# Adjacency tiles kept only in the passes that read them, three more page buffers and a fourth round of first pages in a two-layer graph and expert kernel

## The chip, the cores and the metric

The kernel runs on one core of a Trainium2 chip, in one launch. The metric is the device time of that launch in microseconds (us), taken as the median of a few runs. Times inside the kernel are from one profiled execution, counted from the start of its span. The engines are named as in the profile: PE is the tensor engine (PEld its weight loads), DVE the vector engine, ACT the scalar engine, POOL GpSimd, SP the sync engine, which issues most of the DMA transfers.

## What is computed

The input is 128 graphs of 64 nodes with 256 features, so 8192 rows (`tokens`), and a dense 64x64 adjacency for each graph. Two layers follow each other. Cut to what matters here:

```python
# layer 0
n = layernorm(x);  agg = eps * n + adj @ n
x = x + silu(rmsnorm(agg @ W1 + b1)) @ W2 + b2          # 256 -> 1024 -> 256
n = layernorm(x);  top6 of 64 experts by n @ gate_w.T   # softmax over the six scores
x = x + LN(n + (sum_k score_k * n @ lattice[expert_k]) @ out_w.T + out_b)
# layer 1
n = layernorm(x);  h = LN(n)
x = x + n + relu((adj @ h) @ W_rel + b_rel + h @ W_root)
n = layernorm(x);  top2 of 8 experts
x = x + sum_k p_k * (relu(n @ W1[e_k] + b1[e_k]) @ W2[e_k] + b2[e_k])
```

All of it is in float32. The adjacency is used twice, once in each layer, and the expert sums are sparse: each row goes to six of 64 matrices of 256x256 in layer 0, and to two of eight two-step networks in layer 1.

## The kernel before

The rows are worked on in 32 blocks of 256 (`NB`, two tiles of 128 rows, four graphs). There are four passes, each a `staggered` loop that writes out the order of PE, DVE and ACT by hand (`manual_schedule`); the order of SP's transfers is the scheduler's.

**Layer 0, dense and routing.** For each block `load0` (L787) brings the rows and `load_adjacency` (L745) the four transposed adjacency matrices, as two 64x64 corners of a 128x128 tile for each of the two tiles. `aggregate`, `hidden`, `scale` and `project` make the dense part. Then `choose`, `count` and `slots` give every row its six experts and a place in each expert's list, and GpSimd scatters copies of the row to the table `r0x` in memory (`Router.send`, L419, six copies of two tiles for each block). The last sends end at 614.87 us.

**Layer 0's pages.** An expert's list is read in pages of 128 rows. `page_table` (L443) makes the order of pages on the device: first up to `R` full pages of every expert in turn, then the other full pages, then what is left over, with small rests as half pages. `R` is 3 (the argument of the router before the tuple of likely counts, L977). Twelve pages (`EARLY`) go ahead in buffers of their own (`early0` to `early5`, L1079). Then `run` (L1200) works through 188 pairs of pages and 7 pairs of half-page groups: `fetch` (L1138) loads a pair into a `px` buffer, of which there are 22 (L1140), up to twelve pairs ahead of its use in program order; `flip` transposes it on PE; `apply` (L1173) multiplies by the expert's matrix and DVE scales the result back into the same `px` buffer (L1192); `Router.reply` (L426) lets GpSimd scatter each page's results to the rows of the answer table `r0y`. A `px` buffer is free again when both replies of its pair have landed. For the first 64 pairs ACT also writes a filler page for an expert (`fill_end`). Behind the usual pages stand two branches with spare pages, entered only if the routing needs them.

**Layer 1, dense and routing.** `load_y` (L1340) loads a block's six answers for each row from `r0y`, 1.57 MB a block, in three `y` buffers, four blocks ahead. `mixture` (L1360) sums and transposes them on PE; `fold` (L1381) lets DVE add two of the six first, for blocks after the seventh. A load of `y` must not overtake the replies that it reads. For the blocks below `READY` (6) the loads are declared independent of the replies of pages from `R` x 64 on (the group `r0last`, L431 and L1346): rows of these first blocks lie at the head of each expert's list, so they are in the first `R` rounds. To make sure, `look_back` (L205) notes after `READY` blocks how many rows each expert has, and `page_table` asks for the spare pages, which end in a wait, if some expert has more than the first rounds hold. Loads for later blocks wait for all replies. `load3` (L1354) brings `x1` and the adjacency again; `convolve_b` (L1474) uses it. Rows go to the experts' table `r1x` by GpSimd (`send1`).

**Layer 1's pages** are the last pass; GpSimd adds their results to the output.

The adjacency tiles: four tiles `at0` to `at3` of 1024 bytes a partition are made once, at L740 to L743, in the pool `const`, which lives for the whole kernel. They are cleared once by GpSimd, since loads write only their diagonal corners, and a block `b` uses tile `b % 4` in both layers. Since the tiles are the same, the loads of layer 1's first four blocks stand, in the program that is built, at the end of layer 0's dense pass in SP's queue.

Of the kernel before, what the change touches and what calls it, by code (L numbers as in the profile page):

```python
# [9 lines left out]
F32 = mybir.dt.float32  # L10
# [9 lines left out]
P = 128  # L20
# [71 lines left out]
def chain(blocks, make, key=None):  # L92

    key = key or make.__name__

    def advance(b, n=1):
        B = blocks[b]
        if key not in B:
            B[key] = make(b)
        for _ in range(n):  # L100
            if next(B[key], B) is B:
                break

    return advance
# [562 lines left out]
def two_layer_gnn_moe_kernel(ctx: ExitStack, tc: tile.TileContext, a: dict, out: bass.AP):  # L667
    nc = tc.nc
    x_in, adjT = a["x"], a["adjT"]
    N, D = x_in.shape  # L670
# [4 lines left out]
    T = 2  # L675
    C = T * P
    NB = N // C
    E0 = a["L0_ffn_lattice_weights"].shape[0]
    H0 = a["L0_gnn_W1"].shape[1]
    KH = H0 // P  # L680
    K0 = 6
    E1, F1, _ = a["L1_ffn_W2"].shape
    EARLY = 12
    READY = 6
    FIRST = 4
    FOLD = 2
    LOOK = 20
# [3 lines left out]
    const = ctx.enter_context(tc.tile_pool(name="const", bufs=1))  # L691
    small = ctx.enter_context(tc.tile_pool(name="small", bufs=3))
    counts = ctx.enter_context(tc.tile_pool(name="counts", bufs=3))
    dram = ctx.enter_context(tc.tile_pool(name="dram", bufs=1, space=bass.MemoryType.DRAM))
# [21 lines left out]
    def load_matrix(pool, name, engine=nc.scalar):  # L716

        t = pool.tile([P, a[name].shape[0] // P, a[name].shape[1]], F32, name="m_" + name)
        engine.dma_start(out=t, in_=a[name].rearrange("(k p) f -> p k f", p=P))
        return t  # L720
# [16 lines left out]


    adjacency = []
    for i in range(4):  # L740
        at = const.tile([P, T, P], F32, name=f"at{i}")
        nc.gpsimd.memset(at, 0.0)
        adjacency.append(at)  # L743

    def load_adjacency(b):  # L745
        at = adjacency[b % 4]
        for g in range(2):
            nc.sync.dma_start(out=at[g * G:(g + 1) * G, :, g * G:(g + 1) * G],
                              in_=adjT[2 * b * T + g:2 * (b + 1) * T:2].rearrange("t m n -> m t n"))
        return at  # L750
# [3 lines left out]
    W = D + 2  # L754
# [20 lines left out]
    with tc.tile_pool(name="c0", bufs=1) as c0, \  # L775
            tc.tile_pool(name="work0", bufs=2) as work, \
            tc.tile_pool(name="ph0", bufs=4, space=PSUM) as ph_pool, \
            tc.tile_pool(name="ps0", bufs=2, space=PSUM) as psum, \
            tc.tile_pool(name="pm0", bufs=1, space=PSUM) as pmix:
        mean = c0.tile([P, P], F32, name="mean")  # L780
        nc.gpsimd.memset(mean, 1.0 / H0)
        route = pmix.tile([P, 2, T, E0], F32, name="route")
# [4 lines left out]
        def load0(b):  # L787
            B = blocks[b]
            B["x"] = x = x_view[:, b % 4 * T:(b % 4 + 1) * T, :]
            nc.sync.dma_start(out=x, in_=by_tile(x_in[ts(b, C), :]))  # L790
            B["at"] = load_adjacency(b)
# [156 lines left out]
        def place(b):  # L948
            send(b, 0)
            if b == READY - 1:  # L950
                r0.look_back()
# [3 lines left out]
        def send(b, k):  # L955

            B = blocks[b]
            r0.release(k, *B["w"], B["xs"])
            r0.send(B["row"], B["xs"], b > LOOK, (k,))
# [14 lines left out]
        aggregate(0)  # L974
        rest = lambda f: lambda b: f(b) if b else None

        r0 = Router(tc, const, small, dram, N, D, E0, K0, T, P, 14 * P, 4, "r0", 3, ((K0 * N // P - EARLY) // 4 * 4 + 4, E0 // 2 - 4), True)  # L977
        r1 = Router(tc, const, small, dram, N, D, E1, 2, T, 2 * P, N, 4, "r1", 1,
                    (N // P // 2 - E1 // 2, E1 // 4, E1 - 1), True, total=out, like=r0)
        assert W == r0.W  # L980
# [1 line left out]
        H, R, Q, V, S, Y = (chain(blocks, f) for f in (choose, residual_a, square_sum, normalize, slots, scale))  # L982
# [133 lines left out]
    with tc.tile_pool(name="wx0", bufs=3, reuse_waits="tile") as wx, \  # L1116
# [20 lines left out]

        def fetch(j):  # L1138
            Q = pairs[j]
            Q["px"] = px = wx.tile([P, 2, W], F32, name="px", bufs=22)  # L1140
            if j >= npair:
                regs["row"] = r0.load(2, 4 * (j - npair), ENG.SP)
                for i in range(4):
                    q, h = i // 2, i % 2 * P // 2
                    r0.fetch_rows(regs["row"][i], px[h:h + P // 2, q:q + 1, :], P // 2)
                return
            for q in range(Q["n"]):
                i = 2 * j + q
                if i % 4 == 0:
                    regs["row"] = r0.load(0, i, ENG.SP)  # L1150
                r0.fetch(i, regs["row"][i % 4], px[:, q:q + 1, :])
# [21 lines left out]
        def apply(j):  # L1173
# [17 lines left out]
            for q in range(n):  # L1191
                nc.vector.tensor_scalar(px[:, q, :D], py[:, q, :], px[:, q, D + 1:D + 2], None, op0=ALU.mult)  # L1192
                r0.reply(2 * j + q, px[:, q, :], px[:, q, :D])


        stages = ((-12, fetch), (0, apply),
                  (-2, lambda j: flip(j) if j < 4 or j >= npair else None),
                  (-3, lambda j: flip(j) if 4 <= j < npair else None))
# [23 lines left out]
    wx = ctx.enter_context(tc.tile_pool(name="wx1", bufs=2, side="right", reuse_waits="tile"))  # L1222
# [102 lines left out]
    with tc.tile_pool(name="c3", bufs=1, reuse_waits="tile") as c3, \  # L1325
# [5 lines left out]
        ln_g, ln_b, gamma, beta, bg = (over[x] for x in ("ln_g", "ln_b", "gamma", "beta", "bg"))  # L1331
        w_rel, w_root = (c3.tile([P, KD, D], F32, name="m_" + x) for x in ("rel", "root"))
        wg = load_matrix(c3, "L1_ffn_Wg")
        one = c3.tile([P, P], F32, name="one")
        nc.vector.memset(one, 1.0)
        blocks = [dict() for _ in range(NB)]
# [3 lines left out]
        def load_y(b):  # L1340
            B = blocks[b]
            B["y"] = y = work.tile([P, T, K0, D], F32, name="y", bufs=3)
            for t in range(T):
                d = nc.sync.dma_start(out=y[:, t],
                                      in_=r0.answer[ts(b * T + t, P * K0), :].rearrange("(p k) d -> p k d", k=K0))
                if b < READY:  # L1346
                    tc.declare_no_dep(d.ins, group="r0last", reason="in the first pages, or waited for above")
# [6 lines left out]
        def load3(b):  # L1354
            B = blocks[b]
            B["x1"] = x1 = work.tile([P, T, D], F32, name="x1", bufs=3)
            nc.sync.dma_start(out=x1, in_=by_tile(x1_dram[b]))
            B["at"] = load_adjacency(b)
# [22 lines left out]
        def fold(b):  # L1381

            B = blocks[b]
            B["n"] = K0
            if b > READY + 1:
                B["n"] = n = K0 - FOLD
                y = B["y"]
                nc.vector.tensor_add(y[:, :, :FOLD], y[:, :, :FOLD], y[:, :, n:])
# [177 lines left out]
        for i in (-4, -3, -2):  # L1566
# [50 lines left out]
            (3, count1),  # L1617
            (4, ahead((-3, lambda: down(-4, 0, (0,))), (-2, lambda: up(-3)))),
            (-3, fold),
            (0, A),  # L1620
            (3, S),
# [27 lines left out]
    with tc.tile_pool(name="pt4", bufs=2, space=PSUM, reuse_waits="tile") as pt_pool, \  # L1649
# [26 lines left out]
        def run(order):  # L1676
            order = tuple(order)
            staggered(len(order), [(lag, lambda n, f=f: f(order[n]))
                                   for lag, f in ((-2, fetch), (0, then(flip1)), (1, finish), (0, then(up)))])
# [44 lines left out]
```

## Time and profile before

| what | value |
|---|---|
| median of three runs | 1968.87 us (1968.59 to 1971.76) |
| the profiled execution, its own time | 1970.99 us |
| its span | 1969.2 us |
| granted clock of PE, mean | 0.973 |
| busy in the span | PE 1852.8, PEld 1613.4, DVE 1146.4, ACT 1002.0, POOL 1134.5 us |
| layer 0, dense and routing: PE until | 583 us |
| layer 0's pages: PE's last product ends | 1097.28 us |
| layer 0's pages: GpSimd's last reply ends | 1131.87 us |
| layer 1, dense and routing: PE until | 1477 us |
| layer 1's pages: last add starts | 1956.42 us |

The page of the profile gives busy time by engine, the same in 40 slices of 49.2 us, and groups of like instructions. A group line names the line of code, the engine, what is written and read, the count, the busy time and the mean of one in ns, then the idle time of the engine just before them and what ended most of it. Windows give the busy time of each engine in a stretch, with the number of instructions in brackets. A wait line reads: who waited, for whom, us in total, how many times, the longest. A timeline line reads: start, duration, engine, line, operation, output and input, how many in a row, and in square brackets the idle time before it and what ended it.

### The profile page before, as it was taken

Reading aid. Unit: us, or ns where it says so; the run is one execution under the profiler, and the core shown is the slowest. Engines: PE = TensorE matmul, PEld = TensorE weight load, DVE = VectorE, ACT = ScalarE, POOL = GpSimd, SP = SyncE. Lnnn points to the kernel's source line nnn. Section 1 sums busy time; section 2 is a strip of 40 time slices with the busy share of each in tenths; the row PEclk is TensorE's granted clock in tenths of the full one; section 3 lists DMA queues with packets and bytes.
Section 4 is the critical chain, followed back from the end, with each engine's and each line's share of the span. In section 5 each row is a group of like instructions: output and inputs, shape, how many; then the busy total and the mean of one; then the engine's idle time right before and its main releaser. Section 6 shows DMA issues by size and latency. Waiting matters only on the chain. (4 is left out here: it accounts for less than half of the span.)

```text
span 1969.2 us, 35306 instructions
## 1 busy us (share of the span) xinstructions
PE 1852.8 (94%) x9906; PEld 1613.4 (82%) x9906; DVE 1146.4 (58%) x4256; ACT 1002.0 (51%) x2047; POOL 1134.5 (58%) x1114
## 2 busy tenths in 40 slices
PE   7999999999966899999999899999987999999996
PEld 6888888888845777888877788888876888888885
DVE  5899999999975333344433379999962222222221
ACT  5888888988841222222222266666642333333332
POOL 1377777777677677777777724444443444434443
PEclk9999999999967999999999899999988999999998
DMA  5134555553376988766666799778425666666653
GB/s 139 63 131 143 164 162 163 159 165 131 118 258 216 301 257 264 213 213 206 207 208 191 295 307 337 272 258 281 155 88 129 161 133 130 131 134 130 129 108 48
DMA packets 253085, 359.49 MB, mean 183 GB/s; under 512 B 53176, under 2 KB 210504, under 8 KB 252880
## 3 DMA queue, kind: packets, MB, share of 16 engines
q1 hardware_dynamic: 175904, 210.74, 36.0%
q0 software_dynamic: 62736, 135.21, 23.2%
q10 hardware_dynamic: 14240, 11.12, 1.8%
q8 instruction: 90, 1.47, 0.3%
q14 instruction: 115, 0.94, 0.2%
HBM read 193.27 MB, written 166.03 MB: 182 GB/s over the span
## 5 line engine op out<-in xcount | busy, mean ns | idle before, releaser
L419 POOL DMA_INDIRECT r0x<-xs,r0row x384 | 388.0, 1010 | 216.2 <-ACT lat L883 113.6
L426 POOL DMA_INDIRECT r0y<-px x390 | 378.7, 971 | 122.9 <-DMA r0y<-px 52.2
L1188 PE MATMUL py<-lat,pxT 128*128 x1616 | 385.6, 383 | 21.0 <-ACT pxT L1162 17.7
L436 POOL DMA_INDIRECT out_x<-py_s,px x131 | 202.8, 1548 | 282.5 <-DVE py_s L1322 179.3
L1192 DVE TENSOR_SCALAR px<-py,px 128x256 f32<-128x256 f32 x390 | 171.0, 480 | 306.9 <-PE py L1188 300.7
L1188 PEld LDWEIGHTS py<-lat,pxT 128*128 128x128 f32 x1616 | 293.1, 191 | 60.3 <-ACT pxT L1162 22.2
L1162 ACT COPY pxT<-pt 128x512 f32<-128x512 f32 x188 | 109.7, 586 | 345.3 <-PE pt L1159 241.0
L1292 ACT ACTIVATE phid<-ph,pw 128x256 f32<-128x256 f32 (+1 forms) x264 | 122.0, 462 | 293.0 <-PE ph L1289 180.4
L419 POOL DMA_INDIRECT r1x<-xs,r1row x128 | 134.9, 1054 | 184.1 <-ACT hn L1432 53.9
L894 PE MATMUL ps<-lat 128*128 128x256 f32 x1024 | 240.0, 383 | 0.0
L858 PE MATMUL ph<-lat 128*128 128x256 f32 x1024 | 233.3, 387 | 2.7 <-DVE lat L881 2.0
L1303 PE MATMUL py<-fw,phid 128*128 (+1 forms) x1016 | 232.7, 382 | 0.0
L1289 PE MATMUL ph<-pxT,pw 128*128 128x256 f32 (+1 forms) x1056 | 227.0, 368 | 0.0
L858 PEld LDWEIGHTS ph<-lat 128*128 128x128 f32 x1024 | 195.9, 194 | 29.8 <-issue 2.4
L894 PEld LDWEIGHTS ps<-lat 128*128 128x128 f32 x1024 | 194.3, 192 | 28.3
L1289 PEld LDWEIGHTS ph<-pxT,pw 128*128 128x128 f32 x1056 | 193.0, 190 | 24.7
L1303 PEld LDWEIGHTS py<-fw,phid 128*128 128x128 f32 x1016 | 189.6, 192 | 23.5
L1314 DVE TENSOR_SCALAR p<-p 128x2 f32<-128x2 f32 (+1 forms) x69 | 12.2, 177 | 218.5 <-ACT p L1313 218.5
L1159 PE MATMUL pt<-ident,px 128*128 128x128 f32 x780 | 120.7, 276 | 11.6 <-DMA px<-r0x 11.6
L1320 DVE TENSOR_TENSOR py_s<-py,pb 128x512 f32<-128x512 f32 (+1 forms) x67 | 44.5, 664 | 143.7 <-PE py L1303 141.4
L1159 PEld LDWEIGHTS pt<-ident,px 128*128 128x128 f32 x780 | 97.3, 142 | 36.1 <-issue 10.9
L881 DVE SCALAR_TENSOR_TENSOR lat<-ph,c_L_gnn_b,rms 128x256 f32<-128x256 f32 x256 | 111.9, 476 | 23.0 <-ACT rms L72 22.9
(337 smaller groups left out, 2966.9 us busy)
## 6 DMA issues: line engine op xcount, KB each, us to landing
y<-r0y SPq DMA_DIRECT2D x64, 768.0 KB
px<-r0x SPq DMA_DIRECT2D x376, 129.0 KB
pw<-in_L_ffn_W1b SPq DMA_DIRECT2D x41, 514.0 KB
x<-x SPq DMA_DIRECT2D x64, 256.0 KB
px<-r1x SPq DMA_DIRECT2D x28, 516.0 KB
r0x<-r0filler ACTq DMA_DIRECT2D x64, 129.0 KB
lat<-in_x SPq DMA_DIRECT2D x32, 256.0 KB
lat<-in_L_ffn_lattice_weights SPq DMA_DIRECT2D x8, 1024.0 KB
```

The source lines that it names most:

```text
L419: i = self.nc.gpsimd.indirect_dma_start(out=self.table[:, :], out_offset=bass.IndirectOffsetOnAxis(ap=row[:, t, k:k + 1], axis=0), in_=xs[ ...
L426: d = self.nc.gpsimd.indirect_dma_start(out=self.answer[:, :], out_offset=bass.IndirectOffsetOnAxis(ap=x[:, self.D:self.D + 1].bitcast(I32 ...
L436: i, d = f"{self.name}add{i}", self.nc.gpsimd.indirect_dma_start(out=self.total[:, :], out_offset=bass.IndirectOffsetOnAxis(ap=x[:, self.D ...
L858: nc.tensor.matmul(ph[:, c, :], lhsT=w1[:, k, ts(2 * j + c, P)], rhs=B["aggT"][:, k, :], start=(k == 0), stop=(k == KD - 1))
L881: nc.vector.scalar_tensor_tensor(hT[:, c, :], B["ph", c // 2][:, c % 2, :], b1[:, c:c + 1], B["rms"], op0=ALU.add, op1=ALU.mult)
L894: nc.tensor.matmul(B["po"][:, t, :], lhsT=B["hT"][:, c, ts(t, P)], rhs=w2[:, c, :], start=False, stop=(t == T - 1 and c == KH - 1))
L1159: nc.tensor.transpose(pt[:, k, ts(q, P)], Q["px"][:, q, ts(k, P)], ident)
L1188: nc.tensor.matmul(py[:, q, :], lhsT=xT[q][:, k, ts(h, P)] if parts == 2 else xT[:, k, ts(q, P)], rhs=lat[:, ds(e, 1), k, :].rearrange("p ...
L1192: nc.vector.tensor_scalar(px[:, q, :D], py[:, q, :], px[:, q, D + 1:D + 2], None, op0=ALU.mult)
L1289: nc.tensor.matmul(ph[c - c0][:, :m], lhsT=w[:, k * F1 + c * P:k * F1 + (c + 1) * P], rhs=Q["xT"][:, k, :m], start=(k == 0), stop=(k == KD ...
L1292: nc.scalar.activation(hid[:, c, :m], ph[c - c0][:, :m], AF.Relu, bias=w[:, KD * F1 + c:KD * F1 + c + 1], scale=1.0)
L1303: nc.tensor.matmul(py[:, t, :], lhsT=Q["hid"][:, c, ts(t, P)], rhs=fw2[:, ds(e, 1), c, :].rearrange("p o d -> p (o d)"), start=(c == 0), s ...
```

## The change

The adjacency tiles become tiles of the pools of the two passes that use them, `c0` in layer 0 and `c3` in layer 1. In layer 1 they are new tiles and are cleared again, by DVE. The pool of page buffers has 25 pairs in place of 22, which takes 3 x 2064 bytes a partition; the tiles took 4 x 1024. `R` of layer 0's router is 4 in place of 3 and `READY` 8 in place of 6; the condition of `fold` is written anew and holds for the same blocks as before.

```diff
-    READY = 6
+    READY = 8
...
     adjacency = []
-    for i in range(4):
-        at = const.tile([P, T, P], F32, name=f"at{i}")
-        nc.gpsimd.memset(at, 0.0)
-        adjacency.append(at)
+
+    def clear_adjacency(pool, engine):
+        for i in range(4):
+            at = pool.tile([P, T, P], F32, name=f"at{i}")
+            engine.memset(at, 0.0)
+            adjacency.append(at)

     def load_adjacency(b):
-        at = adjacency[b % 4]
+        at = adjacency[b % 4 - 4]
...
+        clear_adjacency(c0, nc.gpsimd)
         mean = c0.tile([P, P], F32, name="mean")
...
-        r0 = Router(tc, const, small, dram, N, D, E0, K0, T, P, 14 * P, 4, "r0", 3, ((K0 * N // P - EARLY) // 4 * 4 + 4, E0 // 2 - 4), True)
+        r0 = Router(tc, const, small, dram, N, D, E0, K0, T, P, 14 * P, 4, "r0", 4, ((K0 * N // P - EARLY) // 4 * 4 + 4, E0 // 2 - 4), True)
...
-            Q["px"] = px = wx.tile([P, 2, W], F32, name="px", bufs=22)
+            Q["px"] = px = wx.tile([P, 2, W], F32, name="px", bufs=25)
...
         wg = load_matrix(c3, "L1_ffn_Wg")
+        clear_adjacency(c3, nc.vector)
         one = c3.tile([P, P], F32, name="one")
...
-            if b > READY + 1:
+            if b >= READY:
                 B["n"] = n = K0 - FOLD
```

In the program that is built, PE, ACT and POOL have the same instructions in the same order. DVE has four memsets more at the start of layer 1 and notes `r0seen` two blocks later. On SP the eight adjacency loads of layer 1's first four blocks leave the end of layer 0's dense pass and stand one pair after each `x1` load of blocks 0 to 3; from block 4 on some neighbours change places.

## The prediction

> **What bounds the kernel now.** I read the page's slices first. From slice 11 to 22 GpSimd (POOL) stands at 7 in every slice while TensorE (PE) is not always full; after that PE is full and POOL low.
>
> ```profile
> PE   7999999999966899999999899999987999999996
> ...
> POOL 1377777777677677777777724444443444434443
> ...
> L426 POOL DMA_INDIRECT r0y<-px x390 | 378.7, 971 | 122.9 <-DMA r0y<-px 52.2
> ```
>
> The third line is the page's group of replies: GpSimd scatters each finished page of layer 0 to its tokens' rows, 390 times. Busy 971 ns each; the timeline shows one starting every 1.275 us (1128.35, 1129.62, 1130.90), with 0.30 us between them that never shrinks. So a 7 in the slices is a full GpSimd. Next, the stage in windows (columns: window, PE, PE weight load, VectorE, ScalarE, POOL, PE clock, DMA share, GB/s):
>
> ```profile
> 700.00:750.00 50.00, 45.52 (x244) 38.81 (x243) 17.54 (x40) 11.70 (x20) 38.11 (x40) 1.00 0.87 262
> ...
> 850.00:900.00 50.00, 50.00 (x279) 44.10 (x278) 20.34 (x47) 13.65 (x24) 38.10 (x40) 1.00 0.66 206
> ...
> 1000.00:1050.00 50.00, 45.40 (x241) 38.09 (x240) 17.53 (x40) 11.71 (x20) 38.05 (x40) 1.00 0.69 210
> ```
>
> POOL makes 40 replies in each 50 us. A page costs PE six records (two transposes, four products), so PE makes 279/6 = 46.5 pages where it is free, and 40 where it isn't. PE thus gains on POOL from 800 to 970 us and is then held to POOL's pace. What holds it is in the waits of SP's queue between 680 and 1060 us, which fetches the pages:
>
> ```profile
> SPq L652 <- DMA r0y<-px: 168.6, 126, 4.0
> ```
>
> The fetch of pair j waits for the replies of pair j-22, because the `px` buffer is read by them. Counting fetches and replies in the timeline up to one moment, fetches are 39 to 42 pages ahead of replies at every tenth microsecond from 680 to 1060 (22 pairs are 44 pages), and finished pages are ahead of replies by 6 at 800, 19 at 890, 30 at 970, then 30 to 32 until 1080: a full window. The end of the stage, from the timelines of PE, SP and POOL:
>
> ```profile
> 1090.21 7.07 PE L1188 MATMUL py<-lat,pxT 128*128 x32
> ...
> 1097.65 0.83 SPq L1344 DMA_DIRECT2D y<-r0y  x2
> ...
> 1102.53 2.79 PE L1367 MATMUL ps<-ident,y 128*128 128x128 f32 x12 [5.24 <-DMA y<-r0y]
> ...
> 1125.20 1.53 PE L1367 MATMUL ps<-ident,y 128*128 128x128 f32 x12 [0.87 <-DMA y<-r0y]
> ...
> 1130.90 0.97 POOL L426 DMA_INDIRECT r0y<-px  x1 [0.30 <-issue]
> ...
> 1137.49 0.80 SPq L1344 DMA_DIRECT2D y<-r0y  x2
> ```
>
> PE ends its pages at 1097.28, layer 1 starts at once (first `y` load 0.37 us later), and POOL replies on to 1131.87, under layer 1. So the path that sets the time runs: POOL's replies, one buffer window, PE's last page, layer 1. POOL's own end is not on it, except through the `y` load at 1137.49, which waits for the last reply to land (POOL's next instruction waits for the same until 1137.54). From 1125.2 to 1400 PE is full but for 0.14 us.
>
> **What the Trainium skill says.** "Perfetto Trace Analysis", Optimization Strategy: the same gap repeated over a stretch can mean too few buffers for the next tile. The trace agrees: the 126 waits above. "DMA: Bandwidth & Descriptors", Issuing engines are not separate DMA queues: transfers of SP, ScalarE and GpSimd share the same 16 DMA engines. Agrees: with `y` loads and replies together the DMA share is 1.00 to 1.05 in each 5 us window from 1100 to 1130. "TensorE: Matmul & The Clock Gate", What's actually happening: an idle PE falls to half clock. Agrees: granted clock 0.53, 0.50, 0.61 in the three windows from 1100 to 1115, after the 5.24 us gap; the change keeps that gap, so it moves along.
>
> **The change, part by part.**
>
> *Three more `px` pairs (22 to 25).* The window grows by 6 pages. Where it was full, each fetch can go 6 replies earlier: 6 x 1.275 = 7.65 us. PE needs 6 pages more lead to use it; at its gain of (31-6) pages in 170 us that takes 41 us, so even without a better start it has it by about 1011, before the last paced pages near 1063. From there PE works without a wait to 1097.28 (half pages), so its end moves to 1089.6. POOL's end stays near 1132: it never starves but for 1.06 + 2.21 us at 675 to 680, when the 22 pairs had only just filled (fetches 41 ahead at 680); more buffers hardly act there. I take 0; the ends are -3.3 (gap gone) and +3 (gap doubled). **-7.65.**
>
> *Four rounds of pages first, `READY` 8.* The order of pages changes (up to four of an expert before the rest), their number does not. Counted from the reference's inputs: 373 pages and 27 halves under either setting, within the 376 and 28 of the usual pass. The guard that would run the spare passes compares rows of the first `READY` blocks with the first rounds: after 8 blocks the fullest expert has 407 rows, under 4 x 128. So no spare pass. `y` of blocks 0 to 7 now waits for the first 256 pages, whose replies were issued by 960. Block 8 is the first to wait for the last reply; its load went at 1147.19 and would go at 1139.5, still after 1137.5. In the kernel before, block 6's late load cost PE nothing (landed 1144, used 1155), so the gain is 0; left at 6, it would be wanted 7.65 us sooner and still be hidden by the three `y` buffers. **0.** The fold keeps its blocks (`b > 7` and `b >= 8` are the same).
>
> *Adjacency tiles, last part of layer 0.* Eight loads (four blocks, two each) leave SP's queue there. POOL's sends run without a break to 614.87 and set that stage's end. **0.** The four tiles now lie at the head of `c0`, so the six early page pairs lie 4096 bytes lower against the old buffers; the wait for a block's sends goes from the fifth early pair to the sixth. PE stood 9.72 us at that wait, but the early replies could not start before 615 (POOL), nor VectorE evict before its page table was done near 611. **0**; if uncovered, at most those 10 us either way, which POOL takes up.
>
> *Adjacency tiles, layer 1.* Four memsets of 128x256 on VectorE, 272 ns each (row L1168; "VectorE: DVE Perf Modes", Zero memsets can be issued as uint32, gives one cycle per element, 267 ns at its 0.96 GHz): 1.09 us, in 17.95 us of VectorE idleness (1099.3 to 1117.2) and ahead of the first adjacency load. **0**, 1.1 if that cover went. The eight loads now stand in SP's queue between the `y` loads: one pair after each of blocks 0 to 3's `x1`, 0.60 us an issue, 4.8 us in all. Worse, transfers of SP and ScalarE take eight completion semaphores in turn and each waits until the transfer eight before has landed. By the new order `y` of block 2 waits for the end of block 0's second half, block 3's for block 1's, and so on. With the landings of before I get issues at 1107.4, 1114.2, 1119.5 and 1125.8 for blocks 2 to 5, instead of 1103.43, 1109.46, 1115.28 and 1121.70. But the DMA engines take `y` first in, first out, back to back: in the trace's packets the first of those blocks start at 1112.27, 1117.00, 1122.50 and 1127.65. With 1 us from issue to first packet (1097.65 to 1098.64) slack remains: 3.9, 1.8, 2.0 and 0.9 us. So the engines don't run dry; behind SP wait only further loads. What stays is the data: 256 packets of 256 bytes a block at 17 to 18 ns over 16 engines, 0.28 us, three blocks of it ahead of block 3's second half, PE's last wait (1125.20). **+0.9**; ends 0 and, with all four slacks missed by 2 us, +8.
>
> *Carrying on.* From 1150 to 1400 PE is full and POOL at 20 to 25 of 50; waits further on (10.55 us at 1487 for layer 1's pages) hang on that stage's own sends and answers. The shift reaches the end.
>
> Sum: -7.65 + 0.9 = -6.75. Span 1969.2 to 1962.45; the profiled execution 1970.99 to 1964.2; it lies 2.1 us over the median, so the median 1968.87 goes to **1962.1**.
>
> **Rivals.** (1) *The shift is only half carried*: layer 1's first `y` loads fall among more replies, or PE's last lead is 3 pages. For: DMA is saturated from 1100. Against: replies run during both starts alike. 1965.5. (2) *The window isn't what paces PE*, so its end stays, with the adjacency data added: 1969.8. Against: the constant 40 pages, and PE below its 46.5 after 970. (3) *Slower*: SP's queue at the start of layer 1 empties the DMA engines. Each `y` block that is issued after the engines are through costs PE the difference plus 1 us; blocks 2 to 6, 2.5 us each, make 12.5, less 7.65: 1973.7. It decides once the dry times pass 7.65 us; block 5's slack of 0.9 us speaks for it, the others against. (4) *POOL's gap at 675 goes too*: 1958.8.
>
> **How the numbers follow.** Chances: the forecast 0.62 (own range 1960.5 to 1964), half carried 0.17, window not the pace 0.10, slower 0.07, gap gone 0.04. The half-carried case lies on both sides of 0.2% (3.9 us, about what a measurement of this kernel tells from none): faster 0.62 + 0.04 + 0.12 = 0.78, the same 0.15, slower 0.07. The range 1958.5 to 1967.5 holds the forecast and cases 1 and 4, and leaves out 2 and 3, 0.17.
>
> **What would show it.** Fetches 45 to 48 pages ahead of replies after 700, finished pages 36 to 38 ahead at 1040; PE's last page near 1089.6 with POOL's last reply still near 1131; first `y` load about 0.4 us after PE's end; `y` of blocks 6 and 7 not waiting for replies; PE's `y` waits in the start together no more than 1 us longer than the 4.6 us after the first one of before; the 10.5 us gap at 1487 the same length, 6.8 us earlier. Wrong it would be if PE's lead stays near 31, if POOL's last reply moves by more than 3 us, or if `y` packets show breaks between blocks.

## The result and the profile after

The changed kernel takes 1965.37 us in the median of 15 runs (1962.04 to 1968.14), the kernel before 1968.91 us (1965.86 to 1972.36, 15 runs). The ratio is 0.9979, with a 95% interval of 0.9971 to 0.9987: 4.1 us faster, between 2.6 and 5.7. Forecast were 1962.1 us, 6.75 us faster. The sign and the range were right; the gain is smaller than the sum said.

The profiled execution of the changed kernel is the fastest of its 15 (1962.04 us, span 1960.3), that of the kernel before lay 2.1 us above its median. The two profiles therefore differ by 8.9 us where the medians differ by 3.5, so some 5.4 us of what they show is chance. They have to be read stretch by stretch. In the measurements of all experiments but the first one below the kernel before itself took 2293 to 2296 us in place of 1969, so each of those is read only against the kernel before measured beside it.

Line numbers of the changed kernel are 3 higher around layer 0's pages and 4 higher in layer 1. From its page, the slices of PE and POOL and the group of replies:

```profile
PE   7999999999957898999999799999988999999996
...
POOL 1377777777677677777777734444444444444443
...
L426 POOL DMA_INDIRECT r0y<-px x390 | 379.4, 973 | 123.8 <-DMA r0y<-px 42.1
```

POOL's row is the same full 7, and a reply costs what it did (973 ns). The slices are too coarse (49 us) to show more. In windows (columns: window, PE, PE weight load, VectorE, ScalarE, POOL, PE clock, DMA share, GB/s):

```profile
700.00:750.00 50.00, 48.22 (x260) 41.23 (x259) 18.69 (x43) 11.70 (x20) 38.10 (x40) 1.00 0.91 263
850.00:900.00 50.00, 50.00 (x278) 44.14 (x278) 20.15 (x46) 13.46 (x23) 37.98 (x40) 1.00 0.67 205
950.00:1000.00 50.00, 50.00 (x279) 44.15 (x278) 20.15 (x46) 13.46 (x23) 38.11 (x40) 1.00 0.70 211
1000.00:1050.00 50.00, 47.92 (x256) 40.27 (x254) 19.28 (x44) 12.29 (x21) 38.10 (x40) 1.00 0.67 205
```

PE now runs free to 1000 us and beyond (279 records, 46.5 pages), and makes 256 records from 1000 to 1050, where it made 241. POOL makes its 40 replies in each window, as before. SP's queue still waits for replies from 680 to 1060 us, 109 times in place of 126:

```profile
SPq L652 <- DMA r0y<-px: 157.0, 109, 3.5
```

Counted in the timeline, fetches are now 44 to 47 pages ahead of replies at each fiftieth microsecond from 700 to 1050 (before: 39 to 42), and finished pages are 39 ahead at 1040 us (before: 30 to 32). The end of the stage:

```profile
1081.93 7.07 PE L1191 MATMUL py<-lat,pxT 128*128 x32
...
1089.46 0.82 SPq L1348 DMA_DIRECT2D y<-r0y  x2
...
1094.45 2.79 PE L1371 MATMUL ps<-ident,y 128*128 128x128 f32 x12 [5.45 <-DMA y<-r0y]
...
1118.32 1.53 PE L1371 MATMUL ps<-ident,y 128*128 128x128 f32 x12 [0.53 <-DMA y<-r0y]
...
1128.11 1.06 SPq L1348 DMA_DIRECT2D y<-r0y  x2
...
1130.08 1.28 POOL L426 DMA_INDIRECT r0y<-px  x1 [0.30 <-DVE bn_mv L59]
```

PE's last page ends at 1081.93 + 7.07 = 1089.00, 8.3 us earlier, POOL's last reply at 1131.36 (before: 1131.87), the first `y` load goes 0.46 us after PE's end, and `y` of block 6 (1128.11) is issued before the last reply. So the mechanism is the one described. Where the two profiled executions differ, by stretch (all from their timelines; each row starts where the one above ends; the last column is a run shown below):

| stretch, us | before | changed | difference | 27 pairs |
|---|---|---|---|---|
| start to the last send's end | 614.87 | 612.84 | -2.03 | 614.10 |
| to the first reply from a `px` buffer | 15.65 | 15.88 | +0.23 | 18.97 |
| to PE's last page | 466.77 | 460.28 | -6.49 | 458.03 |
| to the first mixture (first `y` wait) | 5.24 | 5.45 | +0.21 | 5.62 |
| to layer 1's pages | 384.73 | 384.01 | -0.72 | 386.20 |
| to the end | 481.90 | 481.80 | -0.10 | 481.89 |
| span | 1969.2 | 1960.3 | -8.9 | 1964.8 |

The window acts in the third row. There the two profiles differ by 6.5 us, not 7.65. The row also holds the new order of pages, which no run at this pace takes apart from the window, and its share of the 5.4 us of chance isn't known. The 2.0 us of the first row, where the change does next to nothing, are luck of these two executions or an effect that no run separates. PE's last page owes 1.8 us of its 8.3 to the first two rows, and counted from the last send POOL's last reply comes later, not earlier: after 518.5 us in place of 517.0.

### The profile page after: what moved, and what is told of

It is laid out like the page before. It is cut to its first block, busy times and chain, and to the rows that moved or that the text cites. A ratio compares the mean times of both kernels' runs of the same rounds, so it can differ in the third digit from the quotient of the medians.

```text
span 1960.3 us, 35296 instructions
## 1 busy us (share of the span) xinstructions
PE 1848.6 (94%) x9906; PEld 1614.7 (82%) x9906; DVE 1147.9 (59%) x4260; ACT 1002.0 (51%) x2047; POOL 1133.1 (58%) x1114
```

## The experiments

The question was which term hides the 1 to 4 us between the sum (6.75) and the measurement (2.6 to 5.7): the window itself, the adjacency loads in layer 1, or the new order of pages.

### 27 pairs, the one run at the usual pace

The changed kernel with two `px` pairs more and two `pxT` tiles fewer (at all three places that ask for one):

```diff
-        ring = [wx.tile([P, KD, C], F32, name="pxT", bufs=5)]
+        ring = [wx.tile([P, KD, C], F32, name="pxT", bufs=3)]
...
-            Q["px"] = px = wx.tile([P, 2, W], F32, name="px", bufs=25)
+            Q["px"] = px = wx.tile([P, 2, W], F32, name="px", bufs=27)
```

> The changed kernel with 27 px pairs, room for the two more made by three pxT tiles in place of five. Where POOL is the pace (PE at full clock, as in the kernel before's profile), 4 pages more of window are worth up to 4 x 1.275 = 5.1 us if PE gains them in time: it was 39 pages ahead of POOL at 1040 us of 45 possible in the changed kernel, so I expect 3 to 5 us and PE's last page near 1084 to 1086. If three pxT tiles are too few for PE, its pages take longer and PE's last page comes after 1089. Where the clock is low (0.92, as in the four runs before) POOL has gaps, PE is the pace and the window is worth nothing: PE's last page 3 us ahead of POOL's last reply.

One execution each: 1966.6 us, the kernel before beside it 1969.05. PE's last page ends at 1091.10, not at 1084 to 1086: the expectation missed. The timelines of SP and POOL say why:

```profile
623.50 1.98 SPq L652 DMA_DIRECT2D px<-r0x  x4
...
628.46 0.97 POOL L426 DMA_INDIRECT r0y<-early  x1 [0.30 <-issue]
633.07 0.97 POOL L426 DMA_INDIRECT r0y<-px  x1 [3.63 <-DVE px L1195]
```

SP's queue waited, from 590 to 860 us:

```profile
SPq L652 <- DMA r0y<-early: 9.2, 2, 7.9
```

In the changed kernel the first `px` fetch goes at 618.59 and POOL passes from the early pages to the `px` pages after 0.53 us:

```profile
628.72 0.97 POOL L426 DMA_INDIRECT r0y<-px  x1 [0.53 <-DVE px L1195]
```

With three `pxT` tiles the first `px` tile moves 4096 bytes down, onto two early pages, and its fetch waits 7.9 us for their replies; POOL idles 3.63 us. (In the two later kernels whose first `px` tile lies in a gap, SP has no wait for early replies, with three `pxT` tiles as well.) Once started, the deeper window does act: fetches are 49 to 51 pages ahead from 750 us on, and the stretch from the first reply to PE's last page is 458.03 us, 2.25 shorter than with 25 pairs and 8.74 shorter than with 22. So at this pace the stage follows the depth (22, 25, 27 pairs: 466.8, 460.3, 458.0 us, one profile each), but with 6.5 and 8.7 us gained against 22 pairs, where 1.275 us a page would make 7.65 and 12.75. With 27 pairs PE had not used all of its room: it was 37 pages ahead at 1050 us and still gaining. It worked without a wait to the end of the paced stretch:

```profile
1000.00:1050.00 50.00, 50.00 (x279) 44.14 (x278) 20.36 (x47) 13.48 (x23) 38.09 (x40) 1.00 0.68 207
```

In this window it made 241 records with 22 pairs, 256 with 25 and 279 with 27, while POOL made 40 replies each time: that is the plainest sign that the depth holds PE back. It also speaks against the other case of the expectation, that three `pxT` tiles are too few for PE.

Part of what is missing shows at 680 to 710 us, where the window first fills. The kernel before, the changed one and the one with 27 pairs (columns as above):

```profile
680.00:690.00 10.00, 10.00 (x56) 8.83 (x55) 3.85 (x9) 2.34 (x4) 7.56 (x9) 1.00 0.90 278
690.00:700.00 10.00, 10.00 (x58) 8.83 (x57) 4.38 (x10) 2.34 (x4) 7.55 (x9) 1.00 0.88 269
700.00:710.00 10.00, 7.26 (x39) 6.00 (x38) 2.63 (x6) 2.34 (x4) 7.56 (x9) 1.00 0.79 238
```

```profile
680.00:690.00 10.00, 9.36 (x52) 7.97 (x51) 3.50 (x8) 2.34 (x4) 7.56 (x9) 1.00 0.98 296
690.00:700.00 10.00, 10.00 (x58) 8.89 (x57) 4.38 (x10) 2.93 (x5) 7.56 (x9) 1.00 0.98 318
700.00:710.00 10.00, 10.00 (x57) 8.82 (x57) 3.94 (x10) 2.34 (x4) 7.56 (x9) 1.00 0.88 257
```

```profile
680.00:690.00 10.00, 7.76 (x44) 6.60 (x43) 2.76 (x8) 1.76 (x3) 6.66 (x7) 1.00 0.98 309
690.00:700.00 10.00, 8.10 (x43) 6.57 (x41) 3.44 (x8) 2.34 (x4) 6.94 (x9) 1.00 0.99 312
700.00:710.00 10.00, 10.00 (x57) 8.78 (x56) 3.55 (x10) 3.03 (x6) 7.66 (x8) 1.00 1.00 313
```

The deeper the window, the longer it takes to fill: fetches reach their full lead over replies (41, 45 and 50 pages) by 680, 690 and 710 us. Meanwhile the DMA engines are full (share 0.90, 0.98 and 0.98 in the first row of each), and PE is short of pages: its first full 10 us after 670 start at 680, 690 and 700. With 22 pairs it then drops again, to 7.26 us from 700 to 710. POOL's gaps between 660 and 700 us, beyond 1.275 us from reply to reply, sum to 3.9, 4.6 and 5.6 us. This is one profile each, the 0.7 us between the first two is of the size of chance, and the run with 27 pairs began its fetches 4.9 us later, which delays its filling too. So that the deeper window itself starves PE and POOL here is likely, not shown.

### Each part alone, and other depths

These kernels were to split the change. The window and the adjacency move without the order of pages (the changed kernel with this edit):

```diff
-    READY = 8
+    READY = 6
...
-        r0 = Router(tc, const, small, dram, N, D, E0, K0, T, P, 14 * P, 4, "r0", 4, ((K0 * N // P - EARLY) // 4 * 4 + 4, E0 // 2 - 4), True)
+        r0 = Router(tc, const, small, dram, N, D, E0, K0, T, P, 14 * P, 4, "r0", 3, ((K0 * N // P - EARLY) // 4 * 4 + 4, E0 // 2 - 4), True)
...
-            if b >= READY:
+            if b > READY + 1:
```

The adjacency move alone: the same, and

```diff
-            Q["px"] = px = wx.tile([P, 2, W], F32, name="px", bufs=25)
+            Q["px"] = px = wx.tile([P, 2, W], F32, name="px", bufs=22)
```

The order alone is the first of these edits the other way round, made to the kernel before. A smaller window is the kernel before with

```diff
-            Q["px"] = px = wx.tile([P, 2, W], F32, name="px", bufs=22)
+            Q["px"] = px = wx.tile([P, 2, W], F32, name="px", bufs=19)
```

These four were measured side by side:

> The change with its order of pages undone (three first rounds and READY 6 as before; adjacency moved, 25 px pairs). Sum on record: the order is worth 0, so this run is 6.75 us below the kernel before in its profile and as far below it as the changed kernel is (measured there: 4.1 us, 2.6 to 5.7). If the four first rounds cost what the changed kernel's median lacks (2.6 us), this run is 6 to 7 us below. If READY 6 is wanted with the longer lead, y of blocks 6 and 7 waits for the last reply and PE shows a wait before them: 2 us or less below. PE's last page near 1089 to 1090 in all three.

> Only the adjacency move: 22 px pairs, three first rounds, READY 6. Sum on record: +0.9 us (ends 0 and +8), PE's last page unchanged near 1097. Rival: the eight loads between layer 1's first y loads, or the wait that moves from the fifth early pair to the sixth, cost 3 to 4 us in most executions and are what the median lacks: +3 to +4 us.

> Only four first rounds and READY 8: adjacency held throughout, 22 px pairs. Sum on record: 0 (within 1.5 us), PE's last page near 1097 and POOL's last reply near 1132. Rival: the other order of pages costs 2 to 3 us, with PE's or POOL's page stage longer by that. A gain of 1 to 2 us would say that y of block 6 did wait in the kernel before.

> The kernel before with 19 px pairs in place of 22, nothing else. If one window of replies paces PE: six pages less, 6 x 1.275 = 7.65 us later, PE's last page near 1105, POOL's last reply near 1132, fetches 34 to 36 pages ahead of replies. If the window is worth only what the changed kernel's median showed, 4 to 5 us later. If it isn't the pace, 0. If the bend at 650 to 700 us (POOL short of pages) also depends on the depth, POOL's last reply moves too.

The changed kernel itself and three of these again:

> The changed kernel itself, for a second profile and a tighter ratio. If the profiled pair on record was typical: 7 to 9 us below the kernel before, PE's last page near 1089. If its median tells the truth: about 4 us below, and the profile shows where the rest goes. The candidate is POOL short of pages between the early pages and 700 us, since the run with 27 pairs had its first px reply 3.6 us after the last early one and 6.2 us of gaps after that (the kernel before 0.3 and 4.2): then POOL's last reply, counted from the last send, comes 2 to 4 us later than in the kernel before (517.0 us), and PE's last page with it.

> Only the adjacency move, at full clock this time: 22 px pairs, three first rounds, READY 6. Sum on record: +0.9 us (ends 0 and +8), PE's last page unchanged near 1097. Rival: the loads among layer 1's first y loads, or the wait that moves from the fifth early pair to the sixth, cost 3 to 4 us in most executions and are what the median lacks.

> Only four first rounds and READY 8, at full clock: adjacency held throughout, 22 px pairs. Sum on record: 0 (within 1.5 us). Rival: the other order of pages costs 2 to 3 us in the page stage, for example by POOL's gaps at 650 to 700 us.

> The kernel before with 19 px pairs in place of 22, at full clock. If one window of replies paces PE and nothing else moves: 7.65 us slower, PE's last page near 1105, POOL's last reply near 1132. If a deeper window also makes POOL short of pages at 650 to 700 us (transfers crowd each other there), POOL's last reply comes 1 to 3 us sooner with 19 pairs and the loss is only 4 to 6 us.

Then the run with 27 pairs with the early pages laid so that the first `px` tile falls into a gap (the edit to that run), and the adjacency alone once more:

```diff
-        for j in (0, 3, 2, 1, None, 4, 5):
+        for j in (0, 1, None, 2, 3, 4, 5):
...
-                ex.tile([P, 1008], F32, name="space")
+                ex.tile([P, 1016], F32, name="space")
```

> The changed kernel with 27 px pairs and three pxT tiles, as in the run with 27 pairs, whose first px tile lay over early pages: its first fetch waited 7.9 us for their replies (623.50 in place of 618.59). Here the early pages are laid in another order (0, 1, gap, 2, 3, 4, 5), so that the first px tile lies in the gap. If that wait was what the run with 27 pairs lost, the first fetch goes near 618.6, POOL's last reply comes near 1131 to 1133, PE's last page near 1085 to 1087, and the time is 8 us below the kernel before (5 to 10), 3 to 4 below the changed kernel. If a deeper window costs what it brings by crowding the transfers at 650 to 700 us, POOL's last reply stays at 1135 or later and the time is only 3 to 4 us below the kernel before. At a low clock: no difference, PE's last page 3 us ahead of POOL's last reply.

> Only the adjacency move: 22 px pairs, three first rounds, READY 6. At full clock, by the sum on record, +0.9 us (ends 0 and +8), PE's last page near 1097. Rival: the loads among layer 1's first y loads cost 3 to 4 us in most executions and are what the changed kernel's median lacks (2.6 us); then PE's waits at the start of layer 1 together are 3 us longer than in the kernel before.

And the window alone, 25 pairs in the kernel before, with no other part of the change (and three `pxT` tiles at all three places):

```diff
-        for j in (0, 3, 2, 1, None, 4, 5):
+        for j in (0, 1, 2, None, 3, 4, 5):
...
-                ex.tile([P, 1008], F32, name="space")
+                ex.tile([P, 2, W], F32, name="space")
...
-        ring = [wx.tile([P, KD, C], F32, name="pxT", bufs=5)]
+        ring = [wx.tile([P, KD, C], F32, name="pxT", bufs=3)]
+        wx.tile([P, 24], F32, name="pad", bufs=1)
...
-            Q["px"] = px = wx.tile([P, 2, W], F32, name="px", bufs=22)
+            Q["px"] = px = wx.tile([P, 2, W], F32, name="px", bufs=25)
```

> The window alone, with nothing else of the change: the kernel before with 25 px pairs, room for the three more made by three pxT tiles in place of five (and a pad of 96 bytes, with the early pages laid 0, 1, 2, gap, 3, 4, 5, so that the first px tile lies in the gap). Adjacency held throughout, three first rounds, READY 6. Against the changed kernel it leaves out the adjacency loads among layer 1's first y loads and the order of pages. If the window is worth its 7.65 us and the rest of the change costs what the changed kernel's median lacks: 7 to 8 us below the kernel before, 3 to 4 below the changed kernel. If the deeper window itself brings only 4 us in most executions (POOL short of pages for longer at 650 to 700 us): 4 us below the kernel before, with POOL's last reply 2 to 4 us later after the last send than the 517.0 us of the kernel before. If y of blocks 6 and 7 is wanted before the last reply has landed, PE shows a wait of 1 to 5 us near 1145. PE's last page near 1089 to 1091 in all.

| kernel | pairs | median, us | ratio to before (95%) | fetches ahead of replies, pages | finished pages ahead |
|---|---|---|---|---|---|
| window 19 | 19 | 2293.39 | 1.0004 (0.9976 to 1.0032) | 33 to 37 | 1 to 5 |
| window 19, again | 19 | 2288.86 | 0.9982 (0.9953 to 1.0010) | 32 to 36 | 0 to 4 |
| order only | 22 | 2290.62 | 0.9993 (0.9965 to 1.0021) | 37 to 43 | 0 to 5 |
| adjacency only | 22 | 2294.33 | 0.9962 (0.9918 to 1.0006) | 37 to 42 | 0 to 4 |
| adjacency only, again | 22 | 2291.19 | 1.0001 (0.9973 to 1.0029) | 38 to 42 | 0 to 4 |
| adjacency only, third | 22 | 2297.59 | 1.0007 (0.9979 to 1.0036) | 38 to 42 | 0 to 4 |
| window and adjacency, no order | 25 | 2292.81 | 1.0025 (0.9990 to 1.0061) | 44 to 46 | 0 to 5 |
| the changed kernel, again | 25 | 2290.44 | 0.9980 (0.9947 to 1.0013) | 44 to 47 | 0 to 4 |
| window alone | 25 | 2293.58 | 1.0009 (0.9976 to 1.0041) | 44 to 48 | 0 to 4 |
| 27 pairs, new layout | 27 | 2299.61 | 1.0036 (1.0011 to 1.0061) | 47 to 52 | 0 to 2 |

The leads are counted in the timelines at each fiftieth microsecond from 950 to 1350. The order alone, again, gave 0.9891 (0.9818 to 0.9964), but that ratio rests on two executions and isn't read.

As experiments on the split they failed: an interval of 0.3% is 7 us here, and effects of 1 to 4 us can't be told from nothing. As experiments on the window they say something that was expected as one case of several (19 pairs), and for executions like these with 27 pairs: no gain from its depth is seen. Fetches run ahead as deep as the buffers allow, some 34 pages with 19 pairs and 50 with 27, but finished pages don't: POOL answers them as they come, and PE's last page ends 3.04 us ahead of POOL's last reply at every depth, where it was 34.6 us (22 pairs), 42.4 (25) and 45.4 (27) ahead at the usual pace. In the second run of 19 pairs a loss of 7.65 us would be a ratio of 1.0033, which lies outside its interval.

The changed kernel in such an execution, in windows (layer 0's dense part, its pages, layer 1's dense part, layer 1's pages):

```profile
200.00:300.00 100.00, 79.99 (x384) 67.89 (x382) 66.16 (x242) 63.35 (x121) 53.78 (x52) 0.90 0.36 115
1000.00:1100.00 100.00, 78.38 (x394) 66.44 (x393) 28.14 (x67) 17.88 (x33) 62.92 (x66) 0.94 0.61 178
...
1500.00:1600.00 100.00, 100.00 (x646) 88.44 (x644) 93.33 (x454) 66.98 (x147) 46.06 (x50) 1.00 0.92 317
1900.00:2000.00 100.00, 100.00 (x507) 88.53 (x506) 23.55 (x71) 36.16 (x88) 42.09 (x28) 1.00 0.64 135
```

What POOL's replies waited for in it from 900 to 1350 us, and after it the same row of the changed kernel's first profile, 700 to 1060 us:

```profile
POOL r0y L426 <- DVE px L1195: 76.7, 54, 2.7
```

```profile
POOL r0y L426 <- DVE px L1195: 16.8, 55, 0.3
```

Layer 1 runs at its usual pace; layer 0 doesn't. In the pages PE makes 66 pages in 100 us (394/6), where it made 93 in the first profile (556 records from 900 to 1000 us), and POOL, which made 79 there, waits for VectorE up to 2.7 us at a time, where in the first profile the longest wait is the 0.3 us between any two replies. What holds PE up is in the timeline of the slower execution:

```profile
1045.09 0.59 ACT L1165 COPY pxT<-pt 128x512 f32<-128x512 f32 x1 [1.62 <-PE pt L1162]
...
1046.57 0.60 PE L1162 MATMUL pt<-ident,px 128*128 128x128 f32 x4
...
1050.90 0.60 PE L1162 MATMUL pt<-ident,px 128*128 128x128 f32 x4
...
1052.95 0.58 ACT L1165 COPY pxT<-pt 128x512 f32<-128x512 f32 x1 [7.28 <-PE pt L1162]
...
1053.59 1.99 PE L1191 MATMUL py<-lat,pxT 128*128 x8 [2.10 <-ACT pxT L1165]
1055.11 2.44 DVE L1195 TENSOR_SCALAR px<-py,px 128x256 f32<-128x256 f32 x6 [4.93 <-remote]
1055.22 1.56 ACT L1165 COPY pxT<-pt 128x512 f32<-128x512 f32 x3 [1.68 <-remote]
```

The transposes of a pair end at 1047.17; ScalarE, idle, starts their copy 5.8 us later, PE waits for it, and VectorE then works off six pages in one go. In the profile of the kernel before, from 900 to 920 us, each of these copies starts 0.09 us after its transposes. The case shown is no exception: of the 118 copies of pairs behind the first 70, counted in the timelines, 38 start more than 1 us after their transposes with ScalarE idle, the latest after 9.7 us, and these come about every 13 us; in the changed kernel's first profile none is more than 0.4 us late. Why ScalarE and VectorE start late in layer 0 and not in layer 1 the records don't say ("remote" is a releaser outside them), and no run here asks.

Two things can still be read from these profiles. First, layer 1, undisturbed, with the adjacency loads among its first `y` loads (six profiles) and without (five): PE's waits ahead of `y` in the first 45 us, the first one left out, sum to 2.5, 3.5, 2.9, 4.8, 3.3 and 4.1 us with, and to 2.0, 2.7, 1.7, 3.6 and 1.5 us without. The means are 3.5 and 2.3: the loads cost **1.2 us**, about 1 either way by the scatter. From the first mixture to layer 1's pages the means are 381.5 and 380.2, the same difference. (In these runs few replies are left when layer 1 starts, so that the DMA engines are less crowded than at the usual pace. There the sums are 4.6 without the loads and 4.4 and, with 27 pairs, 6.9 with them: between nothing and 2.3 us, so 1.2 isn't confirmed there.) Second, 27 pairs in the new layout is the only kernel here whose interval lies wholly on the slower side, by 2.5 to 14 us. Its stage has 121 us of gaps between replies beyond 1.275 us, the others have 105 to 114; whether three `pxT` tiles are too few when ScalarE's copies come in bursts is open, since the window alone, with three as well, has 112.

Whether the new layout or the window alone beats the changed kernel at the usual pace wasn't measured.

## Why the prediction came out as it did

**What paces PE: right.** The fetches went ahead by the six pages (44 to 47), PE's lead grew from 30-32 to 39 pages, and PE's last page now comes 42.4 us ahead of POOL's last reply, where it came 34.6 us ahead. That the two moments fit the forecast so closely (1089.00 for 1089.6, 1131.36 for "near 1132") is luck: the stage began 1.8 us earlier in this execution, and without that they would lie near 1090.8 and 1133.2. The rival that the window isn't the pace falls at the usual pace, and holds where ScalarE and VectorE start late: there the lead on which the window's worth rests never builds up.

**The window's size: too large.** The step took six pages by 1.275 us at full worth, and 0 for the gap at 675 us, "more buffers hardly act there". It counted gaps of 1.06 and 2.21 us there and left out one of 1.56 us at 670.04. The stretch from the first reply to PE's last page shrank by 6.49 us, not 7.65. About 0.7 us of the difference stands at 660 to 700 us, as more starved POOL, within the +3 that the step named as its upper end but on the side it didn't choose; 0.4 us has no place. All of this is of the size of chance between two executions.

**Adjacency tiles in layer 1: right within the scatter.** Forecast +0.9, measured 1.2 between profiles of the slower executions; in the pair of profiles at the usual pace it is covered by scatter (waits after the first 4.4 us, before 4.6). The memsets are there, four of 272 ns from 1090.67 on, in an idle VectorE. The completion semaphores, taken in turn, did delay `y` of blocks 2 to 5, to 1099.78, 1106.24, 1113.90 and 1119.32, and their first packets followed 3.7, 3.6, 1.9 and 2.6 us later (forecast from the old landings: 4.9, 2.8, 3.0 and 1.9): the engines were still busy with earlier blocks, they did not run dry, and the slower rival, which needed that, falls.

**Order of pages, `READY` 8, early pairs: no cost seen.** The order alone is at 0.9993 (0.9965 to 1.0021), which is too wide to exclude 2 us. `y` of block 6 no longer waits for the last reply; that it gains or saves anything was not shown.

**Carrying on: right.** From the first mixture to the end the two profiles differ by 0.8 us; PE's wait before layer 1's pages is 10.99 us (10.55 before).

With the sizes that were read from profiles the sum is -6.5 + 1.2 = -5.3 us, inside the interval of 2.6 to 5.7; it joins one pair of executions at the usual pace to others at the slower one, so it is an estimate. The median of 1965.37 is what the rival "half carried" gave (1965.5), but not for its reason: the start of layer 1 lost no more than about the 1.2 us of the loads, and PE's lead was not cut to half. How much of the remaining 1 us is real stays open, and so does how the 4.1 us divide among the parts, since the split was not measured at the usual pace.

## What to carry to other kernels

A window of buffers that a slower engine frees is worth at most its extra pages times that engine's cadence, and here only while the faster engine really ran ahead: count finished items ahead of the consumer, not fetches, before pricing it, and take something off, because the deeper window also takes longer to fill. The Trainium skill ("Perfetto Trace Analysis", Optimization Strategy) reads a gap that repeats as possibly too few buffers; the runs with late copies show gaps in PE at every depth, so the check is the lead, not the gap. When tile sizes or counts of a pool change, look where the first tiles of the next stage come to lie: a first tile moved by 4096 bytes cost POOL some 3 us in the run with 27 pairs.

## What was not expected of the hardware

ScalarE and VectorE can start several us (in the case shown 5.8) after what they wait for, again and again through one part of a program (layer 0: the pages at 66 in 100 us in place of 93) and not through the next (layer 1: 481 to 482 us for its pages in all profiles). With that the whole launch takes 2290 us in place of 1966, and a gain of 4 us by deeper buffering can't be seen. And more prefetch may lengthen the time in which prefetch itself starves the reader: with 22, 25 and 27 pairs the window was full by 680, 690 and 710 us, with the DMA share at 0.90, 0.98 and 0.98 from 680 to 690 us. That is three single profiles, the last with a late start. It fits what the Trainium skill states in "DMA: Bandwidth & Descriptors", Issuing engines are not separate DMA queues: fetches of SP and replies of GpSimd share the same 16 engines.
